# The correlation's gram in four groups of 32 tokens, two blocks in a row

## The chip, the cores and the metric

The kernel runs on one core of one Trainium2 chip, which works through all eight images by itself. The metric is the device time of one execution in microseconds, and the time of a kernel is the median of its runs.

## The reference, cut to what matters

The input `x` has 8 images of 768 channels by 32 x 32 positions (tokens), in float32. Two layers follow each other, each adding its result to its input.

```python
x = x + _L0_conv_ref(_gn(x), W_qkv, W_proj, b_proj)      # layer 0
    # qkv = tokens @ W_qkv.T ; 12 heads of 64
    # var_v, var_k = variance of v, k over the 64 of a head
    # attn = softmax(var_v @ var_k.T * 64**-0.5) ; out = attn @ v ; out @ W_proj.T + b_proj
x = x + _L1_conv_ref(_gn(x), conv_w, conv_b)             # layer 1
    # feat_n = feature / max(norm over channels, 1e-12), padded by 3 on each side
    # corr[o] = sum over channels of feat_n shifted by offset o, times feat_n
    #   28 offsets of a 7 x 7 window: diagonal, column, antidiagonal, row
    # out = conv_w (1x1) @ concat(feature, corr) + conv_b
```

`_gn` is a group normalisation over 32 groups. The change is in `corr`: each position's inner products over the 768 channels with its neighbours at up to three rows and three columns away.

## The kernel before, in words

**The order of the work.** The program is written out by Python. A planner (class `Clock`) keeps a planned time; every unit of matmuls passes it by a fixed number of microseconds (`KV_US` 1.93 for 12 matmuls of 384 columns, `STEP_US` 1.73 for one step of the attention, `GRAM_US` 1.4 for a gram block), and jobs for the other engines are put at a planned time with `later.after(us, job)`. That decides the order in which the instructions of each engine, and the DMAs of SP's one queue, stand. The engines run by that order and wait for each other's data by semaphores.

**The stages.** The loop `for b in range(NB + 1)` interleaves, in stage b, the attention of image b (layer 0) with the second half of its key and value products (`kv.units(1)`), and with the correlation and 1x1 convolution of image b-1 (layer 1). `work_off` takes attention steps when they are ready and units of the list `rest` otherwise; the gram blocks of image b-1 stand in a second list, `beside`, of which `next_to` starts one at two fixed places of `rest` and before and after each group of attention steps, and `remaining` what is left. The list `rest` then goes on with the convolution.

**The attention.** Twelve heads are six pairs. For each pair ACT makes the exponentials `ex` (L774) of 8 blocks of 128 tokens for both heads, from a row of values `bc` that SP loads as 512 KB (L763), and for some pairs it makes them once more in the other orientation only for their sums (`junk`, L784, from rows `bk`). TensorE multiplies them with the values (`av`, L800). Six `ex` buffers exist, three steps of two heads, so an exponential of step t+3 waits for the `av` of step t. Keys, values, projection and convolution are products by a scheme with fewer multiplications, recorded as `x`, `y`, `z`, `own` at L350; their sums of operands (`s`, L636 to L642) are made by POOL. For other pairs the denominators come from a product with ones, `den` (L831), with four groups of 32 columns.

**The correlation, class `Corr`.** A block is 128 tokens, that is 4 image rows of 32, and there are 8 blocks (`t`) to an image.

- `turn` (L1129 to L1142): POOL copies a block's features so that tokens of the left half of the image rows, and of the right, stand together: two copies of 128 x 384. The tile comes from a pool with one buffer (`turnpool`). Each gram turns the next block. The last image does it on ACT instead, two blocks ahead.
- `gram` (L1144 to L1181): for each of 6 channel slices and each side, one matmul with the turned tokens of that side (64) as the stationary operand and a window of 7 image rows by 19 columns (133; 76 for the last block, where the image ends) as the moving one. In float32 the profile shows each as two records, 24 for a block. The result `ps` is one of two PSUM buffers that it shares with the small transposes: `ptv`, `ptk` (the variances), `it`, `ct` (the correlation).
- `out`: DVE copies `ps` to `win`, and SP writes `win` to DRAM (`windowed`) in two DMAs, one for each side, each 4 image rows x 16 tokens x 136 elements, with a pitch such that a shift of the window becomes a fixed step.
- After blocks 3 and 7, `diagonals` (L1189) reads the products that are wanted back as four DMAs into `dd`, token by token; `scale` makes `m` (DVE) and the reciprocal root `rn` (POOL, L1205), `columns` makes `dn` (DVE), `to_dram` transposes it on TensorE (`ct`, L353), copies it (`cr`), and writes `rows` (L1226).
- `gather` (L1232): 14 DMAs read the rows and the shifted reciprocal norms into `cs` (named `u` in the code) and `v`, which has its own buffer (`uvpool`, 28 x 1024); `product` multiplies them, and three DMAs copy `cs` to the other partition groups. Convolution units then add `cs` with `cc` (L1276, and L1374 in the last image).

Of the kernel before, what the change touches and what calls it, by code (L numbers as in the profile page):

```python
# [6 lines left out]
F32 = mybir.dt.float32  # L7
AF = mybir.ActivationFunctionType
ALU = mybir.AluOpType
# [4 lines left out]
P = 128  # L14
NB, C, H, W = 8, 768, 32, 32
N = H * W
J = C // P
NH, HD = 12, 64
HP = NH // 2
MT = N // P  # L20
HF = N // 2
# [6 lines left out]
RUNS = ((0, 0, 4), (31, -1, 3), (62, -2, 5), (93, -3, 7))  # L28
HW = W // 2
TALL, WIDE = MT // 2 + 3, HW + 3  # L30
AHEAD_OF = [o for first, _, count in RUNS for o in range(first, first + count)][1:]
NA = len(AHEAD_OF)
PAD = 99
SPAN = TALL * WIDE
WIN = SPAN + 3
PITCH = WIN + 3
# [4 lines left out]
NS = len(CHANNELS)  # L41
NCH = 2 * NS + 4
# [11 lines left out]
TAIL = 0.0  # L54
EXP, SUM, STEP_US = 1.07, 1.15, 1.73
KV_US, T_US, CORR_US = 1.93, 2.58, 1.2
GRAM_US = 1.4
WARM, BRIDGE = 42, (3, 7)


# [26 lines left out]
def windows(ap, *dims):  # L87

    return bass.AP(tensor=ap.tensor, offset=ap.offset, ap=[list(d) for d in dims])


class Clock:


    def __init__(self):
        self.now, self.count, self.jobs = 0.0, 0, []
        self.act, self.rows, self.poll = 0.0, ([], []), lambda: None
        self.dve = 0.0

    def after(self, us, job):  # L100
        self.count += 1
# [71 lines left out]
def two_layers(ctx, tc, x, wkv, wproj, bproj, wconv, wcorr, bconv, out):  # L173
    nc = tc.nc

    def pool(name, bufs, **kw):
        return ctx.enter_context(tc.tile_pool(name=name, bufs=bufs, **kw))
# [10 lines left out]
    bcpool = pool("bcpool", 4)  # L188
    bkpool = pool("bkpool", 2)
    expool = pool("expool", 2 * AHEAD)  # L190
    turnpool = pool("turnpool", 1)
    wk = pool("wk", 3)
    uvpool = pool("uvpool", 1)
    st = pool("st", 1)
    xbank = pool("xbank", 2, space=PSUM)
    ybank = pool("ybank", 2, space=PSUM)
# [5 lines left out]
    clock = Clock()  # L202
    later = clock
    vector = Vector(nc.vector, clock)
    ready = set()
# [197 lines left out]
    for j in range(J):  # L403
        for hf, queue in enumerate((nc.sync, nc.scalar)):
            at = slice(hf * HF, (hf + 1) * HF)
# [18 lines left out]
    for base, sign in ((0, 1), (3, -1)):  # L424
        nc.gpsimd.affine_select(
            out=group, in_=group, compare_op=ALU.is_ge, fill=0.0, base=base,
# [16 lines left out]
    cs = const.tile([P, 3, HF], F32, name="cs")  # L443
# [681 lines left out]
    class Corr:  # L1125
# [3 lines left out]
        def turn(self, t):  # L1129
# [7 lines left out]
            for side in range(2):  # L1137
                if last:
                    act_copy(0.5, to[:, :, side], rows[:, :, :, side, :])
                else:  # L1140
                    half = rows[:, :, :, side, :]
                    nc.gpsimd.tensor_tensor(to[:, :, side], half, windows(ones, ones.ap[0], (0, J), (HW, 4), (1, HW)), ALU.mult)  # L1142

        def gram(self, t):  # L1144

            b = self.b
            tall = min(TALL, H - 4 * t)
            n = tall * WIDE
            if t not in self.turned:
                self.turn(t)  # L1150
            block = self.turned[t]
            ps = other([P, SPAN], f"gr{b}_{t}")
            for j in range(J):
                image = self.f[:, j, :].rearrange("p (y x) -> p y x", x=W)
                for side in range(2):
                    left = side * (HW - 3)
                    nc.tensor.matmul(  # L1157
                        ps[side * HD : (side + 1) * HD, :n].rearrange("p (y x) -> p y x", x=WIDE),
                        lhsT=block[:, j, side, :],
                        rhs=image[:, 4 * t : 4 * t + tall, left : left + WIDE],  # L1160
                        start=j == 0, stop=j == J - 1,
                    )
            for ahead in range(t + 1, min(t + (3 if b == NB - 1 else 2), MT)):
                if ahead not in self.turned:
                    self.turn(ahead)

            def out():
                win = wins[t % 2 if t < MT - 1 else 2]
                if b < NB - 1:
                    vector.tensor_copy(win[:, :n], ps[:, :n])  # L1170
                else:
                    act_copy(0.3, win[:, :n], ps[:, :n])
                for side in range(2):
                    to = windowed[b % 2][t : t + 1, side * (HD * PITCH + HD - 3) :]
                    nc.sync.dma_start(
                        out=windows(to, (HW * PITCH - 3, 4), (PITCH, HW), (1, WIN)), in_=win[side * HD : (side + 1) * HD, :]
                    )
                if t % 4 == 3:
                    later.after(4.0, lambda: self.diagonals(t // 4))

            later.after(GRAM_US + 0.25, out)  # L1181

        def diagonals(self, hf):

# [47 lines left out]
        def gather(self):  # L1232

            b, r = self.b, rows[self.b % 2]
            u = cs.rearrange("p a n -> p (a n)")[0:NCH, 0:N]
            v = uvpool.tile([NCH, N], F32, tag="uv", name=f"v{b}")
            nc.sync.dma_start(out=v[NS:NCH, :], in_=windows(r[0:1, PAD:], (0, NS + 4), (1, N)))
            nc.sync.dma_start(out=u[2 * NS : NCH, :], in_=windows(r[1:2, PAD:], (0, 4), (1, N)))
            for n, (first, apart) in enumerate(PICKED):
                k, row = 3 * n, 2 + AHEAD_OF.index(first)  # L1240
                nc.sync.dma_start(out=u[k : k + 3, :], in_=windows(r[row : row + 1, PAD:], (apart * ROW, 3), (1, N)))
                nc.sync.dma_start(out=v[k : k + 3, :], in_=windows(r[0:1, PAD + first :], (apart, 3), (1, N)))
                nc.sync.dma_start(
                    out=u[NS + k : NS + k + 3, :],
                    in_=windows(r[row : row + 1, PAD - first :], (apart * (ROW - 1), 3), (1, N)),
                )

            def product():
                vector.tensor_tensor(u, u, v, ALU.mult)
                vector.tensor_tensor(cs[0:NCH, 2, :], cs[0:NCH, 0, :], cs[0:NCH, 1, :], ALU.subtract)  # L1250
                for n in range(1, 4):
                    nc.sync.dma_start(out=cs[n * FOUR : n * FOUR + NCH, :, :], in_=cs[0:NCH, :, :])
                later.after_dve(6.0, lambda: ready.add(("cs", b)))

            later.after(18.0 if b < NB - 1 else 12.0, product)
# [136 lines left out]

    def remaining(beside):
        while beside:
            next_to(beside)

    def next_to(beside):

        if beside and ready.issuperset(beside[0][1]):
            us, _, unit = beside.pop(0)  # L1400
            unit()
            clock.pass_time(us)
# [19 lines left out]

    def turn_first():
        start_corr(0)
        later.after(6.0, lambda: ready.add("turned"))

    def project(b, ots, held=None):
        f = first_f[0] if b == 0 else layer1[b - 1][0]
# [110 lines left out]
    def start_corr(b):  # L1539
        corrs.append(Corr(b, layer1[b][0]))  # L1540
        corrs[-1].turn(0)

    second, corrs = [], []
    later.after(26.0, lambda: sum_weights(1, 9.0, 1.5))
# [4 lines left out]
    for b in range(NB + 1):  # L1549
# [8 lines left out]
        if b:  # L1558
            has_f = ("f", b - 1),
            if b > 1:  # L1560
                clock.wait(*has_f, ready=ready)
            f, acc = layer1[b - 1] if b > 1 else first_f * 2
            corr = corrs.pop() if 1 < b < NB else Corr(b - 1, f) if b == NB else None
            conv = Conv(
                b - 1, f, images[b] if b < NB else acc, (lambda b=b: next_image(b + 1)) if b + 1 < NB else lambda: None
            )
            if b < NB:

                def low_residual(b=b, f=f):
                    for n in range(JH):  # L1570
                        later.after(1.5 * n, lambda n=n: nc.sync.dma_start(out=f[:, n, :], in_=xv[b, :, n, :]))

                conv.then = low_residual
            grams = [(GRAM_US if t < MT - 1 else 0.9, has_f if b > 1 else has_f + ("turned",), lambda t=t: (corr or corrs[0]).gram(t)) for t in range(MT)]
            first, start = (0.0, has_f, conv.sums.first), (0.0, (), conv.start)
            if b < NB:
                beside = grams
                for n in (3, 7) if b > 1 else (7, 11, 15):
                    rest.insert(n, (0.0, has_f, lambda: next_to(beside)))
                rest.insert(len(rest) - 4, (0.0, has_f, lambda: remaining(beside)))  # L1580
                rest.insert(len(rest) - 4, first)
                rest += [start] + conv.units()
                if b == NB - 1:
                    rest.insert(len(rest) - 3, (0.0, (), conv.set_aside))
            else:
                units, parts = conv.units(), conv.corr_units()
                rest += [first, start] + units[:2] + grams + units[2:17]
                for n, unit in enumerate(units[17:]):
                    rest += parts[n : n + 1] + [unit]
        else:  # L1590
            more = [(us, (("xn", 1),) * (n > 1), unit) for n, (us, _, unit) in enumerate(kv1.units(0))]
            rest.insert(len(rest) - 3, (0.0, (), lambda: apply_second(0)))
            rest += [(0.0, (), lambda: apply_second(1))] + more[:20] + [(0.0, (), lambda: fill_t(3))] + more[20:]
            rest += [(0.0, (), lambda: fill_t(TBLOCKS - 3))]
# [51 lines left out]
```

## Time and profile before

| what | us |
|---|---|
| median of 3 runs | 2581.24 |
| lowest and highest | 2581.23, 2582.12 |
| profiled execution | 2580.07 |
| its span | 2578.3 |
| `gr` (L1157) on the chain that ended last | 3% of the span |
| turns on POOL, 112 copies | 111.0 |
| `win` copies on DVE, 56 | 16.1 |
| product of `cs` and `v` on DVE, 8 | 9.7 |

In the profile, PE is TensorE's matmuls, PEld its weight loads, DVE, ACT and POOL the other engines, and SPq the DMA queue of SyncE. The lines of a timeline have start, length, engine, line of the code, operation, output and inputs, their shapes and a count, and in brackets the idle time before them and what ended it. Matmuls overlap, so the length of a record is not its cost; from the start of a group to the start of the next is. A wait is put down to what came last.

### The profile page before, as it was taken

The numbers are of one execution on the slowest core, as the hardware profiler recorded it, in microseconds if no ns is written. First come the engines' busy times: TensorE is split into PE (matmuls) and PEld (weight loads), VectorE is DVE, ScalarE is ACT, GpSimd is POOL, SyncE is SP. The second block draws the span as 40 slices with busy tenths as digits, with TensorE's granted clock in tenths as the row PEclk, the third lists the DMA queues.
The fourth block names the chain that finished last, engine by engine and source line by source line (L and its number), as shares of the span: only waits on it lengthen the run. The fifth ranks groups of instructions, "written<-read, shape, count | busy, mean of one in ns | idle before, by whom it ended". The sixth has DMA issues, their size and how long they took to land.

```text
span 2578.3 us, 40707 instructions
## 1 busy us (share of the span) xinstructions
PE 2570.6 (100%) x14798; PEld 1345.3 (52%) x14798; DVE 1586.7 (62%) x4101; ACT 1422.0 (55%) x1972; POOL 425.3 (16%) x449
## 2 busy tenths in 40 slices
PE   9999999999999999999999999999999999999999
PEld 5644354434764347643476434764347643575333
DVE  6868735775347853478534885358853577536864
ACT  1497279811697217971179711897118971199610
POOL 4320130004300043000430003300133001331000
PEclk9999999999999999999999999999999999999999
DMA  8866366355563655636556365563655636545333
GB/s 295 291 225 221 103 210 189 119 196 170 184 200 104 198 169 175 206 97 208 168 174 202 98 212 171 168 201 105 221 170 162 206 107 218 163 142 166 119 110 108
DMA packets 324718, 448.19 MB, mean 174 GB/s; under 512 B 59810, under 2 KB 245522, under 8 KB 324518
## 3 DMA queue, kind: packets, MB, share of 16 engines
q1 hardware_dynamic: 322454, 442.24, 53.7%
q10 hardware_dynamic: 2064, 3.34, 0.4%
q8 instruction: 118, 1.93, 0.3%
q14 instruction: 82, 0.67, 0.1%
HBM read 376.70 MB, written 64.40 MB: 171 GB/s over the span
## 4 chain that ended last, share of the span: by engine, by line
PE 99%; DVE 0%; issue 0%; POOL 0%; DMA 0%; ACT 0%; SPq 0%; ACTq 0%; POOLq 0%; DVEq 0%
PE x L350 35%; PE av L800 25%; PE y L350 18%; PE z L350 10%; PE own L350 5%; PE gr L1157 3%; PE den L831 1%; PE warm L419 1%; PE y L1063 0%; PE z L1063 0%; PE cc L1276 0%; DVE acc L167 0%; DMA windowed<-win 0%; POOL turn L1142 0%; PE cc L1374 0%
## 5 line engine op out<-in xcount | busy, mean ns | idle before, releaser
L774 ACT ACTIVATE ex<-bc,nk 128x1024 f32<-128x1024 f32 x768 | 828.9, 1140 | 397.1 <-DMA bc<-vdr 191.0
L800 PE MATMUL av<-ex,v 128*64 128x512 f32 x3072 | 692.4, 593 | 0.1
L800 PEld LDWEIGHTS av<-ex,v 128*64 128x64 f32 x3072 | 337.1, 137 | 311.0 <-issue 182.3
L784 ACT ACTIVATE junk<-bk,vm 128x1024 bf16<-128x1024 f32 x368 | 421.5, 1145 | 26.9 <-issue 10.6
L167 DVE TENSOR_TENSOR acc<-acc,ex 128x1024 f32<-128x1024 f32 x300 | 344.9, 1214 | 0.0
L350 PE MATMUL y<-kv,s 128*64 128x384 f32 x1488 | 265.5, 487 | 0.7 <-POOL s L636 0.7
L350 PE MATMUL x<-kv,xn 128*64 128x384 f32 x1512 | 259.7, 486 | 0.0
L350 PE MATMUL x<-kv,s 128*64 128x384 f32 x1488 | 256.2, 486 | 0.0
L229 ACT COPY kp<-x 128x384 f32<-128x384 f32 x28 | 13.4, 479 | 404.6 <-PE x L350 395.8
L350 PEld LDWEIGHTS x<-kv,xn 128*64 128x64 f32 x1512 | 141.2, 137 | 102.4 <-issue 84.1
L350 PEld LDWEIGHTS x<-kv,s 128*64 128x64 f32 x1488 | 144.1, 137 | 91.6 <-issue 70.5
L350 PEld LDWEIGHTS y<-kv,s 128*64 128x64 f32 x1488 | 139.3, 137 | 87.7 <-issue 70.9
L530 POOL TENSOR_TENSOR rstda<-vea,neghalf 128x1 f32<-128x1 f32 x8 | 4.8, 596 | 947.5 <-DVE vea L167 947.5
L1142 POOL TENSOR_TENSOR turn<-f,ones 128x384 f32<-128x384 f32 x112 | 111.0, 1011 | 242.1 <-PE gr L1157 153.5
L350 PE MATMUL z<-kv,xn 128*64 128x384 f32 x768 | 134.1, 486 | 0.0
L350 PE MATMUL x<-f,wt 128*64 128x512 f32 x504 | 118.5, 593 | 0.0
L167 DVE TENSOR_TENSOR v<-y,v 128x128 f32<-128x128 f32 x180 | 41.0, 284 | 122.9 <-PE y L350 122.9
L636 POOL TENSOR_TENSOR s<-xn 128x384 f32<-128x384 f32 x64 | 66.6, 1051 | 294.0 <-PE x L350 189.1
L167 DVE BATCH_NORM_STATS2 vbn<-v 128x6 f32<-128x64 f32 x720 | 101.9, 213 | 0.0
L350 PEld LDWEIGHTS z<-kv,xn 128*64 128x64 f32 x768 | 75.9, 137 | 46.4 <-issue 36.6
L229 ACT COPY acc<-li 32x256 f32<-32x256 f32 x128 | 51.7, 404 | 82.8 <-DVE li L167 81.4
L1157 PEld LDWEIGHTS gr<-f,turn 128*64 128x64 f32 x1344 | 89.6, 136 | 11.0 <-POOL turn L1142 1.3
(205 smaller groups left out, 3134.0 us busy)
## 6 DMA issues: line engine op xcount, KB each, us to landing
kv<-kvs SPq DMA_DIRECT2D x124, 576.0 KB
kv<-in_wkv_dram SPq DMA_DIRECT2D x95, 576.0 KB
bc<-vdr SPq DMA_DIRECT2D x96, 512.0 KB
f<-in_x_dram SPq DMA_DIRECT2D x48, 512.0 KB
bk<-kdr SPq DMA_DIRECT2D x46, 512.0 KB
x1d<-f SPq DMA_DIRECT2D x42, 512.0 KB
xn<-x1d SPq DMA_DIRECT2D x42, 512.0 KB
out_dram<-xn SPq DMA_DIRECT2D x82, 256.0 KB
```

Source lines behind the costliest of these rows:

```text
L167: return getattr(self.engine, name)(*args, **kw)
L229: nc.scalar.copy(to, at)
L350: nc.tensor.matmul(out[at], lhsT=lhsT[:, at], rhs=rhs, start=start, stop=stop, **kw)
L419: nc.tensor.matmul(warm[:, 0:P], lhsT=ident, rhs=ident, start=True, stop=True)
L530: nc.gpsimd.tensor_tensor(self.rstd, ve, neghalf[:, 0:1], ALU.pow)
L636: nc.gpsimd.tensor_tensor(self.sums[g][:, 0], a[g][2], a[g][3], ALU.add)
L774: nc.scalar.activation(ex, self.bc[e], AF.Exp, scale=self.kv.nk[self.half][:, h, t : t + 1])
L784: nc.scalar.activation(junk, self.bk[e], AF.Exp, scale=self.kv.m2[self.half][:, h, t : t + 1], accum_out=self.sums[:, e, t : t + 1],)
L800: nc.tensor.matmul(self.av[hf][e * HD : (e + 1) * HD, :], lhsT=self.vt[:, t, e, :], rhs=exs[e][:, hf * HF : (hf + 1) * HF], start=t == 0, ...
L831: nc.tensor.matmul(den[at * 32 : (at + 1) * 32, :], lhsT=ones[:, 0:32], rhs=self.acc[e][:, hf * HF : (hf + 1) * HF], start=True, stop=True,)
L1142: nc.gpsimd.tensor_tensor(to[:, :, side], half, windows(ones, ones.ap[0], (0, J), (HW, 4), (1, HW)), ALU.mult)
L1157: nc.tensor.matmul(ps[side * HD : (side + 1) * HD, :n].rearrange("p (y x) -> p y x", x=WIDE), lhsT=block[:, j, side, :], rhs=image[:, 4 * ...
```

## The change

For images 0 to 6 the block of 128 tokens is multiplied in four groups of 32 instead of two of 64: the left and right halves of two image rows each. A group's window needs 5 image rows instead of 7, so the moving operand has 95 columns, and there are twice as many matmuls. The four groups' results stand in four groups of 32 partitions of `ps`, that is in four column groups of the array. Block 7 keeps its 76 columns. The eight blocks are started as four pairs, and a `turned` time in the planner keeps a pair from being started before two turns have had time. There are two turn buffers; turns run two ahead. The window's DMAs are four to a block of 2 image rows x 16 tokens x 98 elements, except for block 7 (two, as before). The tile `v` is now two halves of 512 columns that lie in the two turn buffers, so five loads of the gather become ten, and the product is two multiplications. The last image keeps its two groups and takes over only the halves of `v`. Image 0's grams stand at other places of `rest`.

```diff
+SHORT = 2 + 3
-GRAM_US = 1.4
+GRAM_US, TURN_US = (1.3, 2.4), 3.4
...
-    turnpool = pool("turnpool", 1)
+    turnpool = pool("turnpool", 2)
-    uvpool = pool("uvpool", 1)
...
+        def grams(self, t):
+            clock.turned = clock.now + GRAM_US[1] + TURN_US
+            for n in range(2):
+                self.gram(t + n)
...
+            last = t == MT - 1
+            groups = 2 if b == NB - 1 else 4
+            tall = min(SHORT if groups == 4 else TALL, H - 4 * t)
...
-                for side in range(2):
-                    left = side * (HW - 3)
+                each = P // groups
+                for at in range(groups):
+                    side, low = divmod(at, groups // 2)
+                    left, first = side * (HW - 3), 4 * t + (0 if last else 2 * low)
                     nc.tensor.matmul(
-                        ps[side * HD : (side + 1) * HD, :n].rearrange("p (y x) -> p y x", x=WIDE),
-                        lhsT=block[:, j, side, :],
-                        rhs=image[:, 4 * t : 4 * t + tall, left : left + WIDE],
+                        ps[at * each : (at + 1) * each, :n].rearrange("p (y x) -> p y x", x=WIDE),
+                        lhsT=block[:, j, side, low * each : (low + 1) * each],
+                        rhs=image[:, first : first + tall, left : left + WIDE],
                         start=j == 0, stop=j == J - 1,
                     )
-            for ahead in range(t + 1, min(t + (3 if b == NB - 1 else 2), MT)):
+            for ahead in range(t + 1, min(t + 3, MT)):
...
-                for side in range(2):
-                    to = windowed[b % 2][t : t + 1, side * (HD * PITCH + HD - 3) :]
+                whole = last or groups == 2
+                size, count, down = (WIN, 4, 0) if whole else (SHORT * WIDE + 3, 2, 2 * (HW * PITCH - 3 + WIDE))
+                for first in range(0, P, count * HW):
+                    side, low = divmod(first, HD)
+                    to = windowed[b % 2][t : t + 1, side * (HD * PITCH + HD - 3) + (down if low else 0) :]
...
-            later.after(GRAM_US + 0.25, out)
+            later.after(1.65 if b == NB - 1 else GRAM_US[t % 2] + 0.25, out)
...
-            v = uvpool.tile([NCH, N], F32, tag="uv", name=f"v{b}")
-            nc.sync.dma_start(out=v[NS:NCH, :], in_=windows(r[0:1, PAD:], (0, NS + 4), (1, N)))
+            vs = [turnpool.tile([P, J * P], F32, tag="turn", name=f"v{b}_{hf}") for hf in range(2)]
+            for hf, v in enumerate(vs):
+                nc.sync.dma_start(out=v[NS:NCH, :HF], in_=windows(r[0:1, PAD + hf * HF :], (0, NS + 4), (1, HF)))
...
-                vector.tensor_tensor(u, u, v, ALU.mult)
+                for hf, v in enumerate(vs):
+                    vector.tensor_tensor(cs[0:NCH, hf, :], cs[0:NCH, hf, :], v[0:NCH, :HF], ALU.mult)
...
+            clock.turned = 0.0
             next_to(beside)
...
-        if beside and ready.issuperset(beside[0][1]):
+        if beside and ready.issuperset(beside[0][1]) and clock.now >= clock.turned:
...
-        later.after(6.0, lambda: ready.add("turned"))
+        later.after(8.0, lambda: ready.add("turned"))
...
         corrs[-1].turn(0)
+        corrs[-1].turn(1)
...
-                for n in (3, 7) if b > 1 else (7, 11, 15):
+                for n in (3, 7) if b > 1 else (7,) + tuple(range(12, 30, 2)):
```

More of the change, by code (lines that the diff above doesn't have):

```diff
@@ L97, in __init__ @@
         self.act, self.rows, self.poll = 0.0, ([], []), lambda: None
-        self.dve = 0.0
+        self.dve = self.turned = 0.0
     def after(self, us, job):
@@ L1142, in turn @@
                     nc.gpsimd.tensor_tensor(to[:, :, side], half, windows(ones, ones.ap[0], (0, J), (HW, 4), (1, HW)), ALU.mult)
+        def grams(self, t):
+            clock.turned = clock.now + GRAM_US[1] + TURN_US
+            for n in range(2):
+                self.gram(t + n)
         def gram(self, t):
             b = self.b
-            tall = min(TALL, H - 4 * t)
+            last = t == MT - 1
+            groups = 2 if b == NB - 1 else 4
+            tall = min(SHORT if groups == 4 else TALL, H - 4 * t)
             n = tall * WIDE
@@ L1172, in out @@
                     act_copy(0.3, win[:, :n], ps[:, :n])
-                for side in range(2):
-                    to = windowed[b % 2][t : t + 1, side * (HD * PITCH + HD - 3) :]
+                whole = last or groups == 2
[3 more added lines that the diff above has]
+                    to = windowed[b % 2][t : t + 1, side * (HD * PITCH + HD - 3) + (down if low else 0) :]
                     nc.sync.dma_start(
-                        out=windows(to, (HW * PITCH - 3, 4), (PITCH, HW), (1, WIN)), in_=win[side * HD : (side + 1) * HD, :]
+                        out=windows(to, (HW * PITCH - 3, count), (PITCH, HW), (1, size)),
+                        in_=win[first : first + count * HW, :size],
                     )
@@ L1241, in gather @@
                 nc.sync.dma_start(out=u[k : k + 3, :], in_=windows(r[row : row + 1, PAD:], (apart * ROW, 3), (1, N)))
-                nc.sync.dma_start(out=v[k : k + 3, :], in_=windows(r[0:1, PAD + first :], (apart, 3), (1, N)))
+                for hf, v in enumerate(vs):
+                    nc.sync.dma_start(out=v[k : k + 3, :HF], in_=windows(r[0:1, PAD + first + hf * HF :], (apart, 3), (1, HF)))
                 nc.sync.dma_start(
@@ L1248, in product @@
             def product():
-                vector.tensor_tensor(u, u, v, ALU.mult)
+                for hf, v in enumerate(vs):
+                    vector.tensor_tensor(cs[0:NCH, hf, :], cs[0:NCH, hf, :], v[0:NCH, :HF], ALU.mult)
                 vector.tensor_tensor(cs[0:NCH, 2, :], cs[0:NCH, 0, :], cs[0:NCH, 1, :], ALU.subtract)
@@ L1573, in two_layers @@
                 conv.then = low_residual
-            grams = [(GRAM_US if t < MT - 1 else 0.9, has_f if b > 1 else has_f + ("turned",), lambda t=t: (corr or corrs[0]).gram(t)) for t in range(MT)]
+            if b < NB:
+                keys = has_f if b > 1 else has_f + ("turned",)
+                grams = [(GRAM_US[1], keys, lambda t=t: (corr or corrs[0]).grams(t)) for t in range(0, MT, 2)]
+            else:
+                grams = [(1.4 if t < MT - 1 else 0.9, has_f, lambda t=t: corr.gram(t)) for t in range(MT)]
             first, start = (0.0, has_f, conv.sums.first), (0.0, (), conv.start)
```

## The prediction

> **What bounds the kernel now.** I read the busy row and the chain first. The page's head gives a span of 2578.3 us; the profiled execution took 2580.07 us, 1.8 us around the span, and 1.2 us less than the median, 2581.24. The sum below is made against the 2580.07 and then moved up by 1.2. The granted clock is 1.000.
>
> ```profile
> PE 2570.6 (100%) x14798; PEld 1345.3 (52%) x14798; DVE 1586.7 (62%) x4101; ACT 1422.0 (55%) x1972; POOL 425.3 (16%) x449
> PE 99%; DVE 0%; issue 0%; POOL 0%; DMA 0%; ACT 0%; SPq 0%; ACTq 0%; POOLq 0%; DVEq 0%
> ```
>
> By these, TensorE is everything, and a microsecond taken from it is a microsecond gained. Averages can hide a stage in which a second engine is just as full, so next I read busy time by stretches of one stage (image 3's attention; stages repeat every 318.3 us). Columns: length, then PE, PEld, DVE, ACT, POOL busy, clock, DMA share, GB/s. Then the ACT waits of the first stretch (sum, count, longest), and the two long ones in the ACT timeline (start, length, ..., idle before).
>
> ```profile
> 989.00:1083.10 94.10, 94.10 (x599) 68.61 (x595) 41.05 (x166) 90.15 (x121) 20.16 (x21) 1.00 0.57 180
> 1083.10:1160.00 76.90, 76.90 (x372) 38.86 (x370) 50.71 (x52) 62.46 (x73) 0.00 (x0) 1.00 0.36 112
> ```
> ```profile
> ACT ex L774 <- PE av L800: 3.4, 3, 2.2
> ```
> ```profile
> 991.16 3.24 ACT L774 ACTIVATE ex<-bc,nk 128x1024 f32<-128x1024 f32 x3 [2.19 <-PE av L800]
> ```
> ```profile
> 1006.49 2.19 ACT L774 ACTIVATE ex<-bc,nk 128x1024 f32<-128x1024 f32 x2 [0.93 <-PE av L800]
> ```
>
> From the first `av` (989.0) until the exponentials of the third head pair end (1083.03), ACT works through: 90.15 of 94.10 us, and of the rest it waits 3.4 us in three places for a buffer that an `av` frees. PE reaches the `av` that consumes the last of these within 0.5 us of it. So this stretch has two full engines, and all eight gram blocks lie in it or just ahead of it. After 1083.1 ACT is idle 14.4 of 76.9 us and only PE counts.
>
> **The grams.** A block before is 24 matmul records of 133 columns:
>
> ```profile
> 987.66 1.57 PE L1157 MATMUL gr<-f,turn 128*64 128x133 f32 x23
> 989.02 0.59 PE L800 MATMUL av<-ex,v 128*64 128x512 f32 x1
> ```
> ```profile
> 1030.76 1.05 PE L1157 MATMUL gr<-f,turn 128*64 128x76 f32 x23
> 1031.63 0.49 PE L350 MATMUL x<-kv,s 128*64 128x384 f32 x1
> ```
>
> Start to start, 989.02 - 987.66 = 1.36 us (113 ns for each pair side by side); the short block 0.87. A stage has 7 x 1.36 + 0.87 = 10.4 us of it. After, a block is 48 records of 95 columns, in sets of four. The nearest row of the old trace is the denominators' `den`, 32 columns wide and four side by side:
>
> ```profile
> 525.39 2.85 PE L350 MATMUL y<-f,wt 128*64 128x512 f32 x12
> 528.18 1.06 PE L831 MATMUL den<-acc,ones 128*32 128x512 f32 x8
> 529.17 2.37 PE L350 MATMUL x<-f,wt 128*64 128x512 f32 x10
> ```
>
> Its two sets take 0.99 us from entry to leaving, where two streams of 512 columns take 0.79 to 0.85; singly read starts put the extra cost of going to 32 columns and back at 0.205 us. A pair of blocks then costs 24 sets x (95/133 x 110.8 + 2.5 = 82 ns) + 0.205 = 2.17 us against 2.72, and the last pair, whose second block keeps 76 columns, 1.98 against 2.23. Three pairs and the last save 3 x 0.55 + 0.25 = 1.9 us a stage.
>
> A rule speaks against this: the Trainium skill, "TensorE: Matmul & The Clock Gate", section "Wait — 56ns, not 53.3ns?", says that starts come no closer than about 25 ns, however few columns. Four starts per set would then make 100 ns, not 82, and the pair 24 x 100 + 205 = 2.6 us, saving 0.1. The old trace does not decide: `den` starts its four 7 ns apart, but then rests 430 ns; the densest sustained row is the 76-column block, one start per 33 ns, and that is what its own columns need. If 33 ns were the floor, a pair would take 3.4 us. The other rule, "TensorEngine Tiling (Array Packing)", section "Key Properties", has a change of tiling drain the array; the row prices that at 0.205 us, and running two blocks in a row pays it four times a stage rather than eight. I take P = 2.25 us for a pair, nearest to `den`, and keep 2.1 to 2.6 for the range.
>
> **What the shorter grams are worth in one stage.** The order of both programs' instructions shows the move. Count from T, where the values' transposes start (971.12 here). Before the first `av`: was 3 blocks, 0.4 of transposes and 7 units of 12 matmuls at 1.93, i.e. 4.08 + 0.4 + 13.5 = 17.9 us, as measured (989.02). Now 3 pairs, 0.4 and 6 units: 3P + 12.0, which is 18.45 at P = 2.17 and 18.7 at 2.25. So the first `av` comes 0.5 + 3(P - 2.17) later, and with it ACT's start at 991.16. In return the fifth `av` (t4) is reached sooner: before at 1004.41 = T + 33.3; now four steps of 1.715, transposes `ct` 0.3, last pair 1.98 and two units 3.87 after the first one, i.e. T + 31.5. ACT's wait of 0.93 us there goes. The end of ACT's run thus moves by 0.5 - 0.93 + 3(P - 2.17) = -0.4 + 3(P - 2.17): -0.2 us at P = 2.25, -0.6 at 2.1, +0.3 at 2.4, +0.9 at 2.6. PE, which has 1.6 us less to do, would wait for exponentials (about 0.7 us at the first pair's t7, 0.3 at each of the next two): that is what is late next. Six stages (images 1 to 6): -1.2 us.
>
> Image 0's grams run in a stage where ACT is full too; there PE lost 0.24 and 0.23 us to the single turn tile (`gr` waits for `turn`, 0.5 in all), which a second tile removes. Beyond that, ACT could run on only if its row loads come sooner, too; I take -0.8, between 0 and -1.5. Image 7 keeps its grams.
>
> **The other parts.** *Turns*: POOL does the same 16 of 1.97 us each, two ahead; after the ones that follow the maximum at 968.6 it starts at 976.26. By walking the queue, turns 2 and 3 end at T + 9.1 and PE wants them at T + 9.5: 0.4 us of cover. POOL is 16% busy; moving turns ahead of the `s` sums pushes these by 2 to 4 us, under the conv's later use: nothing. *Copies and windows*: eight copies of 0.29 us on DVE as before; SP issues 14 more window DMAs an image, each 16 rows lower but half as many; SP's queue, about 0.3 us an issue, has room except where named below. *Gather and product*: five more loads (0.31 us each on SP = 1.6 us) and the product as two halves of about 0.6 us where one took 1.21; its result is due tens of us later in images 0 to 6. In image 7 the copies of `cs` are now landed by my count near 2559.6 against a use at 2560.45: 0, or +0.8 at worst. *The v tile's own buffer* goes; the turn tiles are idle by then, since the next image's first turn comes a stage later: 0.
>
> Sum: 2580.07 - 1.2 - 0.8 = 2578.1, plus 1.2 to the median: **2579 us**.
>
> **Rivals.** *The gain is kept* (chance 0.17): if ACT's run isn't what ends the stretch, because its waits shrink further when `av` comes sooner, PE's saving stays: 6 x 1.9 + 1.5 = 13 us, 2568. For it: PE busy 100%, chain 99%. Against: the 90.15 of 94.10.
>
> *The windows stand behind the row loads* (0.16, slower). Grams 2 and 3 now come earlier and in a row, and their eight window DMAs stand in SP's queue behind four row loads (`bk`, `bc`, 512 KB each) and ahead of the diagonals, so `dn` is late and PE stands at the first `ct`, now put right after four `av` steps:
>
> ```profile
> 981.83 0.88 SPq L763 DMA_DIRECT2D bk<-kdr  x2
> 982.76 1.42 SPq L763 DMA_DIRECT2D bc<-vdr  x2
> ...
> 1002.05 2.02 SPq L1189 DMA_DIRECT2D dd<-windowed  x4
> ```
>
> Before, `dn` was done at 1008.9 and used at 1012.6, 3.7 us of cover. My walk of the new order has it done at T + 25.05 against a use at T + 25.3: 0.25 left. A wait of x behind that holds `av` t4 and all PE work behind it; the first 1.3 us replace PE's waits for ACT. It breaks even at x = 1.5 and at x = 3 costs 1.7 - 0.2 = 1.5 us in six stages, +9: 2590 us. For it: the windows and the loads meet; against: the planner gave `dn` the same fixed delays, and 2 MB are mostly landed by then.
>
> *Starts are the limit* (0.14): P = 2.6 by the rule gives +0.9 x 6 - 0.8 = +5, 2586; at 2.9, 2591. *It doesn't do what it says*, i.e. four groups run two by two: 48 x 82 ns would be 4 us a pair and +30 us; `den`'s four records within 0.43 us speak against it (0.02).
>
> **How the numbers follow.** ACT-bound, as summed: 0.51, with 2574 to 2584. A measurement of this kernel can tell about 0.2%, 5.2 us, from no change. Faster than 2576: the kept gain 0.17 and 0.08 of the likeliest case, 0.25. Slower than 2586.4: 0.14 of the windows, 0.09 of the starts, 0.02, and 0.02 of the likeliest, 0.27. The rest, 0.48. The range reaches from 2570, in between the likeliest and the kept gain, to 2589, which leaves out some 0.1 on each side.
>
> **What would show it.** A pair of blocks start to start near 2.25 us and its records in fours; 82 ns or 100 ns a set decides the rule. ACT's waits in the stretch: the 0.93 gone, the 2.2 larger by 0.5 to 0.8; new waits of `av` for `ex` on PE, about 1.3 us a stage. `ct` waiting for `dn` shows the slower rival. A stage that shrinks by 1.9 us with no PE wait would prove me wrong about ACT, and one that grows with P at 2.2 wrong about SP's queue.

## The result, and the profile after

The changed kernel takes 2624.18 us (median of 6 runs, 2622.47 to 2629.13) against 2581.23 (2579.92 to 2582.12): a ratio of 1.0171, 95% interval 1.0161 to 1.0182, 43 us slower. I had said 2579, and 2570 to 2589. The profiled execution took 2628.18 us with a span of 2626.5; 5.0 us of its surplus lie ahead of the first image's transposes, where its granted clock was one half for 6.8 us as in no other profiled run, and have no part in what follows.

Busy time and chain first:

```profile
PE 2585.6 (98%) x16142; PEld 1188.4 (45%) x16142; DVE 1599.3 (61%) x4109; ACT 1418.1 (54%) x1972; POOL 421.9 (16%) x449
PE 90%; DMA 4%; DVE 3%; ACT 1%; SPq 1%; issue 1%; POOL 0%; DVEq 0%; ACTq 0%
```

PE's part of the chain was 99% before; it has left a tenth of it to others, above all DMA and DVE. Its waits (us in total, times, longest) name the place; before, all its waits together were under 4 us:

```profile
PE ct L353 <- DVE dn L168: 27.6, 12, 3.8
PE ct L353 <- DVE win L168: 3.0, 1, 3.0
```

The twelve waits for `dn` are two in each of the six stages of images 1 to 6. PE's timeline of image 2's correlation, in the stage that the prediction read:

```profile
1000.08 2.17 PE L1167 MATMUL gr<-f,turn 128*32 128x95 f32 x96
1002.18 7.09 PE L800 MATMUL av<-ex,v 128*64 128x512 f32 x32
1012.62 0.69 PE L353 MATMUL ct<-ident,dn 128*64 128x128 f32 x4 [3.35 <-DVE dn L168]
1013.24 2.97 PE L1167 MATMUL gr<-f,turn 128*32 128x95 f32 x96
1016.14 2.16 PE L350 MATMUL y<-kv,s 128*64 128x384 f32 x12
```

The pair of gram blocks takes 1002.18 - 1000.08 = 2.10 us. Behind four `av` steps PE stands 3.35 us at `ct`. The next pair, one of whose blocks is shorter, takes 2.90 us. The windows around it say why (length, busy times, granted clock, DMA share, GB/s):

```profile
1008.00:1012.00 4.00, 1.27 (x6) 0.14 (x2) 0.81 (x5) 4.00 (x6) 1.06 (x1) 0.99 0.30 13
1012.00:1016.00 4.00, 3.38 (x100) 3.09 (x100) 1.02 (x6) 3.97 (x6) 0.00 (x0) 0.58 0.10 24
1016.00:1020.00 4.00, 4.00 (x40) 1.80 (x30) 1.69 (x10) 2.54 (x5) 0.00 (x0) 1.00 0.09 22
```

After standing, PE runs at half its clock. Apart from the drop at the start, the clock record has one at the first `ct` of every stage from image 0 to image 6: five of 3.4 us and two of 6.8 us; before there was none inside the span. What `dn` waited for is in SP's queue:

```profile
994.20 2.75 SPq L1188 DMA_DIRECT2D windowed<-win  x4
996.99 0.91 SPq L763 DMA_DIRECT2D bk<-kdr  x2
998.09 1.79 SPq L763 DMA_DIRECT2D bc<-vdr  x2
1000.03 2.43 SPq L1188 DMA_DIRECT2D windowed<-win  x4
1008.16 2.03 SPq L1203 DMA_DIRECT2D dd<-windowed  x4
```

Gram 3 was done at 994.1. Its windows were issued at 1000.03, behind gram 2's and the 2 MB of row loads, and `dd`, which reads them back, could only start at 1008.16. Before, `dd` could start at 1002.05, with gram 3's windows issued 4.1 us ahead of it:

```profile
997.95 1.09 SPq L1175 DMA_DIRECT2D windowed<-win  x2
```

And ACT, of which I had said that it would be what PE meets, waits more for PE rather than less (6.8 us from the first `av` to 1100, against 3.4 in the stretch before):

```profile
ACT ex L774 <- PE av L800: 6.8, 3, 3.4
```

### The profile page after: what moved, and what is told of

It reads as the page before. It is cut to its first block, busy times and chain, and to the rows that moved or that the text cites. A ratio compares the mean times of both kernels' runs of the same rounds, so it can differ in the third digit from the quotient of the medians.

```text
span 2626.5 us, 43625 instructions
## 1 busy us (share of the span) xinstructions
PE 2585.6 (98%) x16142; PEld 1188.4 (45%) x16142; DVE 1599.3 (61%) x4109; ACT 1418.1 (54%) x1972; POOL 421.9 (16%) x449
## 4 chain that ended last, share of the span: by engine, by line
PE 90%; DMA 4%; DVE 3%; ACT 1%; SPq 1%; issue 1%; POOL 0%; DVEq 0%; ACTq 0%
PE x L350 34%; PE av L800 22%; PE y L350 17%; PE z L350 9%; PE own L350 5%; PE gr L1167 2%; DMA windowed<-win 2%; DVE dn L168 1%; PE den L831 1%; DMA dd<-windowed 1%; ACT ex L774 1%; DMA xn<-in_x_dram 0%; DVE v L168 0%; DVE acc L168 0%; DMA bc<-vdr 0%
## 5 line engine op out<-in xcount | busy, mean ns | idle before, releaser
L800 PE MATMUL av<-ex,v 128*64 128x512 f32 x3072 | 704.8, 595 | 1.0 <-ACT ex L774 0.6
L800 PEld LDWEIGHTS av<-ex,v 128*64 128x64 f32 x3072 | 289.3, 137 | 374.3 <-issue 277.4
L350 PEld LDWEIGHTS x<-kv,s 128*64 128x64 f32 x1488 | 133.9, 137 | 107.1 <-issue 95.7
L350 PEld LDWEIGHTS x<-kv,xn 128*64 128x64 f32 x1512 | 119.7, 137 | 125.9 <-issue 111.0
L350 PEld LDWEIGHTS y<-kv,s 128*64 128x64 f32 x1488 | 123.1, 138 | 106.3 <-issue 92.0
L350 PE MATMUL x<-f,wt 128*64 128x512 f32 x504 | 124.2, 593 | 0.0
L168 DVE SCALAR_TENSOR_TENSOR xn<-x,bconv_sb,xn 128x512 f32<-128x512 f32 x63 | 46.4, 745 | 89.4 <-PE x L350 88.8
L350 PEld LDWEIGHTS z<-kv,xn 128*64 128x64 f32 x768 | 64.1, 137 | 60.6 <-issue 50.1
```

What stands on the lines that cost most here:

```text
L168: return getattr(self.engine, name)(*args, **kw)
L350: nc.tensor.matmul(out[at], lhsT=lhsT[:, at], rhs=rhs, start=start, stop=stop, **kw)
L800: nc.tensor.matmul(self.av[hf][e * HD : (e + 1) * HD, :], lhsT=self.vt[:, t, e, :], rhs=exs[e][:, hf * HF : (hf + 1) * HF], start=t == 0, ...
```

## The experiments

The theory after the result: **the loss is the two waits at `ct` and the clock behind the first; they come from the windows' place in SP's queue and from the row loads beside them**. Rivals: the narrow tiles or the narrow windows cost by themselves; the order of the grams and ACT's later start cost; the clock falls for another reason. All times below are medians; the kernel before had 2580.5 to 2581.0 beside them.

**1. Row loads behind gram 3's windows.**

```diff
+                if hp == 1 and self.b > 1 and ("win", self.b - 1) not in ready:
+                    return
...
                 if t % 4 == 3:
+                    ready.add(("win", b))
```

> The changed kernel; only the two bk and two bc row loads of the second head pair (2 MB) are issued behind the windows of gram 3, not ahead of them, for images 1 to 6. Theory A (windows land late because they stand behind the row loads, dn is late, PE stands 3.4 us at the first ct and its clock halves for 3.4 us after that): dn done 4 to 6 us earlier, the first ct waits under 0.5 us, no clock drop in six stages: 2624 - 6 x (3.4 + 1.7) = about 2593, and 2590 to 2598 as the second ct keeps its 1.2 us. Theory B (four window DMAs to a block and 392-byte pieces are slow by themselves, or ct simply stands too early): dn moves by under 1.5 us, the first ct still waits over 2 us: 2612 to 2626.

Measured: 2600.46 us (ratio 1.008, 1.0063 to 1.0096). The edit moved less than I had written: the two `bk` loads belong to the first pair and stayed ahead, so 1 MB of the 2 MB moved. `dn` came 2.4 us earlier, the first `ct` waited 0.6 to 2.05 us (none in one stage), and no clock drop was left in the six stages:

```profile
PE ct L353 <- DVE dn L168: 15.7, 11, 2.0
```

The time is above theory A's 2590 to 2598, and the sizes are smaller than it had them. Its direction holds: with half of the traffic moved, the first waits fell from 19.4 to 7.1 us in sum. Theory B's 2612 to 2626 is out.

**2. `ct` later.**

```diff
-                later.after_dve(0.7 if b else 5.0, lambda: to_dram(dn))
+                later.after_dve(0.7 + (b < NB - 1) * 9.0 if b else 5.0, lambda: to_dram(dn))
```

> The changed kernel with to_dram, and so both ct, planned 9 us later for images 1 to 6 (the first ct now stands between the fifth and sixth av step after the first four). If the waits at ct and the clock drops behind them are the whole loss: no PE wait at ct in six stages, clock 1.000 there, 2624 - 6 x (4.5 + 1.7) = about 2587, and with the 1.1 us a stage that DVE's order costs (v<-v,rd ahead of the first acc) still there. Rival: the loss is in the new order of the grams and ACT's later start, and PE meets ACT instead: 2600 to 2615, waits of av for ex in place of ct for dn.

Measured: 2584.62 us (2581.08 to 2590.16; ratio 1.0017, 1.0009 to 1.0025). No wait at `ct` in the six stages, and 39.6 of the 43 us are gone, though `dn` is as late as in the changed kernel (28.8 us after the values' transposes). PE doesn't meet ACT in their place.

**3. The four groups in the old order.** The kernel before, with the matmuls and the narrow windows of the change only; the diff is the core of it, and the lines that follow from it are those of the change.

```diff
+            groups = 2 if b == NB - 1 else 4
+            tall = min(SHORT if groups == 4 else TALL, H - 4 * t)
...
```

> The kernel before with the four groups of 32 columns and their short windows only: blocks stay single and where they were, one turn tile, v as before. A block should take 12 x 79 ns + 0.2 = 1.15 to 1.2 us against 1.36, so PE loses 1.2 us of work a stage. ACT-bound theory: the first av comes 0.5 us sooner and the end of the stretch follows by 0.3 to 0.6: 2577 to 2580. Gain-kept theory: 7 x 1.2 = 8 us, 2573. Slower theory (narrow tiles or 14 more window DMAs an image cost by themselves): dn late, ct waits, over 2586.

Measured: 2578.35 us (ratio 0.9992, 0.9983 to 1.0). PE's timeline:

```profile
988.38 1.19 PE L1162 MATMUL gr<-f,turn 128*32 128x95 f32 x48
989.50 7.09 PE L801 MATMUL av<-ex,v 128*64 128x512 f32 x32
```

A single block is 1.12 us to the next start, against 1.36, and yet each stage is only 0.37 us shorter. The time lies where the ACT-bound theory had it, but PE itself gives the gain back, around each block. The neighbours of these two blocks, first before the change, then here:

```profile
985.72 2.26 PE L350 MATMUL y<-kv,s 128*64 128x384 f32 x12
995.88 1.57 PE L1157 MATMUL gr<-f,turn 128*64 128x133 f32 x23
```
```profile
986.34 2.10 PE L351 MATMUL y<-kv,s 128*64 128x384 f32 x12
996.51 1.19 PE L1162 MATMUL gr<-f,turn 128*32 128x95 f32 x48
```

The unit ahead of the block takes 2.04 us instead of 1.94, and the four `av` steps between two blocks 7.01 instead of 6.86. A pair of blocks pays this once instead of twice. Neither the narrow tiles nor four window DMAs a block make a loss where they meet nothing: `dn` is done 37.2 us after the transposes, before the change 37.8.

**4. Two groups in the new order.**

```diff
-            groups = 2 if b == NB - 1 else 4
+            groups = 2
```

> The changed kernel with two groups of 64 columns and the two wide window DMAs again; order of work, two blocks in a row, two turn tiles, halves of v stay. A pair costs 2.7 us against 2.1. If the order makes the loss, the first ct still waits 2 to 4 us and the clock still drops: 2624 + 6 x 1.9 = about 2635 (2628 to 2640). If the four narrow window DMAs make it, the waits go: 2624 - 31 + 11 = about 2604.

Measured: 2598.54 us (ratio 1.0072, 1.0057 to 1.0087), below all that I had expected. PE's waits at `ct` for `dn`:

```profile
PE ct L353 <- DVE dn L168: 6.1, 6, 1.4
```

All six are at the second `ct` of a stage. The first one finds `dn` ready, in image 2 by 0.6 us, and the clock never drops. So the order alone takes the cover away and makes the second wait; the first wait needs the four groups in that order. In image 2 they bring `dn` 2.7 us later and PE 1.3 us sooner to `ct`. The windows' part in this: gram 2's two wide ones occupy SP for 1.2 us where the four narrow ones took 2.75; with two the row loads leave sooner, and gram 3's windows are issued at 14.0 rather than 16.6. My "if the order makes the loss" and "if the narrow windows make it" were both too simple; with experiment 3, neither does it without the other.

**5. Windows past SP's queue.**

```diff
-                    nc.sync.dma_start(
+                    (nc.gpsimd if t == 3 and 0 < b < NB - 1 else nc.sync).dma_start(
```

> The changed kernel with the four window DMAs of gram 3 of images 1 to 6 issued by POOL, past SP's queue. If the place in SP's queue is what delays them (behind two bk and two bc loads and gram 2's windows), they start 2 to 3 us sooner and dn is done 2 to 3 us earlier: first ct waits 0.5 to 1.5 us, no clock drop: about 2598 to 2605. If they are slow to land because 2 MB of row loads hold the DMA engines meanwhile, or POOL issues slowly, dn moves by under 1 us: 2618 to 2628.

Measured: 2607.44 us (ratio 1.0102, 1.0089 to 1.0115). POOL issued the four at 991.12, 13.8 us after the transposes:

```profile
991.12 2.60 POOL L1188 DMA_DIRECT2D windowed<-win  x4
```

`dn` came 2 us earlier, the first `ct` waited 0.4 to 1.7 us.

```profile
PE ct L353 <- DVE dn L168: 20.3, 12, 2.6
```

The time is 2 us above the 2605 that I had at most: the second `ct` now waits 1.6 to 2.65 us, and the clock drops behind it in three of the six stages. Passing the queue gives 2 us of `dn`; each window still took 5 to 7 us from issue to landing, and the read-back started 6.9 us after the last issue; before the change it was 3.5. Both are in it, the place in the queue and the slow landing.

That the row loads slow the landing, and not the small pieces of the narrow windows, is read from the other experiments in the same stage. In experiment 1, with half of the loads moved behind, the read-back starts 3.7 us after the last issue. In experiment 4 the two wide windows stand beside the loads, and it is 7.4 us; in experiment 3 the four narrow ones are clear of them, and it is 2.5.

One stage of each kernel (image 2's grams), in us after the values' transposes:

```
                      gram 3 copied   windows issued   dd issued   dn done   ct on PE
before                    26.5          26.8-27.4        30.9        37.8      41.5
changed                   11.2          16.6-18.4        24.7        29.0      29.2
1 rows behind             11.0          13.6-16.9        20.7        26.6      26.7
3 four, old order         26.0          26.3-28.1        30.6        37.2      41.1
4 two, new order          11.9          14.0-14.6        22.0        26.3      26.9
5 POOL's queue            11.7          13.8-15.8        22.7        27.0      27.2
```

**6. The wait filled.** Four matmuls whose result is overwritten stand ahead of the first `ct` (they add work and change no output).

```diff
                 pt = small(f"ct{b}_{hf}")
+                for n in range(4 if hf == 0 and 0 < b < NB - 1 else 0):
+                    nc.tensor.matmul(pt, lhsT=ident, rhs=self.f[:, 0, 0:HF], start=True, stop=True)
```

> The changed kernel with four idle matmuls of 128x512 (3.4 us, their result is overwritten) on PE right ahead of the first ct of images 1 to 6, where PE waited 2.3 to 3.8 us. PE is as late as before but busy. If the halved clock after the wait is a consequence of PE's idling, the clock stays 1.000 in six stages and the time falls by what the drops cost, 6 x 1.7 to 3.4 = 10 to 14 us: 2610 to 2615. If the drop comes from something else (load of other engines, DMA), it stays: 2624 or a little more.

Measured: 2620.02 us (ratio 1.0152, 1.0139 to 1.0165).

```profile
1004.63 3.70 PE L1231 MATMUL ct<-f,ident 128*128 128x512 f32 x8
1008.26 0.44 PE L353 MATMUL ct<-ident,dn 128*64 128x128 f32 x4
1008.63 1.98 PE L1167 MATMUL gr<-f,turn 128*32 128x95 f32 x96
```

No clock drop is left in the six stages, and the last pair is back at 1.91 us from 2.90: the idling causes the drop. But the time fell by 4, not 10 to 14 us. The filler is 0.4 us longer than the mean wait, and PE, no longer slowed, reaches the second `ct` sooner and stands there 1.8 us in the mean where it was 1.4: part of what the half clock cost lay ahead of another wait. In the profiled executions the six stages fell by 5.3 us, and the drop at image 0's `ct`, which has no filler, was 6.8 us long instead of 3.4.

**7. DVE's order as well.** In experiment 2 the stages of images 1 to 5 gained 0.6 to 1.4 us up to the first of two `den`, against the kernel before, and each gave back 1.13 between the two. There DVE's order had moved. Before:

```profile
1119.19 1.21 DVE L167 TENSOR_TENSOR v<-v,rd 128x1024 f32<-128x1024 f32 x1
1125.00 0.69 DVE L167 TENSOR_TENSOR xn<-z,xn 128x512 f32<-128x512 f32 x1 [4.60 <-PE z L1063]
1127.52 2.35 DVE L167 TENSOR_TENSOR acc<-ex,ex 128x1024 f32<-128x1024 f32 x2
```

After the change:

```profile
1142.39 0.69 DVE L168 TENSOR_TENSOR xn<-z,xn 128x512 f32<-128x512 f32 x1 [5.73 <-PE z L1063]
1144.91 1.22 DVE L168 TENSOR_TENSOR v<-v,rd 128x1024 f32<-128x1024 f32 x1
1146.05 2.35 DVE L168 TENSOR_TENSOR acc<-ex,ex 128x1024 f32<-128x1024 f32 x2
```

`v<-v,rd` used to fill an idle stretch; now it stands behind the `xn` operations and ahead of the `acc` that frees ACT's buffers. Nothing in the change names it: the planner's times moved.

```diff
-            self.rd_at = clock.now + {HP // 2: 8.0, HP - 2: 12.0}.get(self.hp, 14.0)
+            self.rd_at = clock.now + {HP // 2: 8.0, HP - 2: 12.0, HP // 2 - 1: 12.0 if self.b else 14.0}.get(self.hp, 14.0)
...
-                later.after_dve(0.7 if b else 5.0, lambda: to_dram(dn))
+                later.after_dve(0.7 + 9.0 * (b < NB - 1) if b else 14.0, lambda: to_dram(dn))
```

> The run with ct later, with two more moves in the plan: the rows for the third head pair count as landed 2 us earlier, which puts v<-v,rd back ahead of the four xn operations in DVE's order as in the kernel before (images 1 to 6), and image 0's ct stand 9 us later as well. If DVE's order costs 1.1 us a stage (the step of +1.13 between two den in each stage) it goes: -6.7 us, and -2 to -4 for image 0's wait of 2.3 us and its clock drop: 2571 to 2577, below both kernels. If ACT is the hidden bound (my prediction's step), the stage cannot shrink below that of before by more than 0.2 to 0.6 us: 2577 to 2582.

Measured: 2582.94 us over 22 runs from 2577.38 to 2591.93 (ratio 1.0009, 1.0003 to 1.0016): a miss in the median, of which I had expected 2571 to 2577. In the profiled execution the step between the `den` is gone; two of the stages are 1.4 us shorter than before, two 0.8 to 0.9. But one is 3.5 us longer. PE's timeline there, and POOL's:

```profile
1656.42 5.78 PE L350 MATMUL y<-kv,s 128*64 128x384 f32 x24 [2.47 <-POOL s L640]
```
```profile
1650.02 1.01 POOL L1219 TENSOR_TENSOR rn<-m,neghalf 128x4 f32<-128x4 f32 x1 [16.12 <-DVE m L168]
1651.00 1.96 POOL L636 TENSOR_TENSOR s<-xn 128x384 f32<-128x384 f32 x2
1652.92 1.95 POOL L638 TENSOR_TENSOR s<-s,xn 128x384 f32<-128x384 f32 x2
1654.83 1.96 POOL L640 TENSOR_TENSOR s<-xn,s 128x384 f32<-128x384 f32 x2
```

The second half's `rn`, which waits for a DMA, stands in POOL's queue ahead of the `s` sums, and PE for `s`; then the clock drops again.

**8. The same with two groups.** Experiment 7 with `groups = 2`.

> The same as the run above it with two groups of 64 columns (and two wide window DMAs) instead of four of 32. If the shorter grams are kept once nothing waits: slower than that run by 7 blocks' worth, 6 to 7 stages x 1.5 = 9 to 11 us, 2580 to 2588. If ACT bounds the stretch, the two differ by 1 to 4 us only, since ACT takes back what PE gains.

Measured: 2583.37 us (2582.49 to 2584.5; ratio 1.0008, 1.0 to 1.0016). The medians differ by 0.4 us, less than either case had, and taken alone would speak for ACT. But experiment 7 has that wait for `s`, and this run has none at L640; by stages the two differ: +0.14 us each in this run against before, -1.39 and -1.40 in the two best stages of experiment 7. The four groups are worth 1.53 us a stage, and in such a stage all of it is kept.

**9. The sums ahead of `rn`.** Experiment 7 with

```diff
-            later.after(6.0, lambda: self.scale(hf, dd))
+            later.after(6.0 + 8.0 * (hf == 1 and b < NB - 1), lambda: self.scale(hf, dd))
```

> The run with ct later and DVE's order mended, with one more move: the scale of blocks 4 to 7 is planned 8 us later (images 0 to 6), so that POOL's rn of that half, which waits for a DMA, stands behind the s sums in POOL's queue as before the change, not ahead of them. If PE's wait of 2.5 us for s in one stage of that run (and a clock drop of 3.4 us behind it) came from this, no stage waits for s at L640, the spread of its times (2577 to 2592) shrinks to some 3 us, and the time is 6 stages x -1.4, with about +1 elsewhere: 2571 to 2576. If the spread has another source (row loads, ACT), it stays, and the median with it near 2580 to 2583.

Measured: 2571.75 us (2571.02 to 2574.62; ratio 0.9966, 0.9954 to 0.9979), 9 us below the kernel before and 52 below the changed one. No wait for `s` at L640. Against before, the first five stages are -1.4 us three times, -0.32 and -1.23, and the sixth runs like the first three as far as its first `it`. The stretch in which I had called ACT full, over the same 94.10 us from its first `av`, and ACT's waits for `av` there:

```profile
986.42:1080.52 94.10, 94.10 (x595) 56.05 (x593) 43.91 (x169) 92.61 (x125) 13.45 (x15) 1.00 0.61 187
```
```profile
ACT ex L774 <- PE av L800: 0.4, 1, 0.4
```

## Why the prediction was wrong, by its steps

**The cost of a pair (right).** 2.10 us to the next start, and units after and before the pair 0.04 and 0.1 us longer: 2.24 with both, where I took 2.25. The first `av` came 18.71 us after the transposes; I had 18.7. A set of four starts every 81.7 ns. That is the line through the old blocks, 113.3 ns a set for 133 columns and 65.9 for 76, at 95 columns. The rule that spoke against it does not hold here: 81.7 ns are 20.4 ns a start, below the 25 that the Trainium skill, "TensorE: Matmul & The Clock Gate", section "Wait — 56ns, not 53.3ns?", gives as the least. The section "Measured speedup vs the span model" of the same page, some 4 ns for each further tile, would have come nearer: 79 ns of columns and 3 x 4 make 91 ns as an estimate, where the other rule makes 100.

**ACT's bound (wrong by 1.2 us a stage).** I let only one of ACT's waits, 0.93 us, give way, and put the stage at -0.2 (for P = 2.25). Experiments 7 and 9 have -1.4 in their best stages, experiment 8 at P = 2.72 has +0.14 where the same formula says +1.25. The slope was right (1.53 us where 3 x 0.47 gives 1.4), the level was not: ACT's waits for `av` were PE's pace showing on ACT, and they shrank from 3.4 to 0.4 us in experiment 9. An engine that is busy for 96% of a stretch and waits only for the bound engine is not a second bound. The rival "the gain is kept" had the mechanism, for a program in which nothing else moves.

**PE's waits for ACT (wrong, and they mattered).** With them I had cushioned the slower rival: "the first 1.3 us replace PE's waits for ACT". In experiment 9, where nothing else holds PE, the whole run has two of them, 0.8 us in all, so each microsecond at `ct` counts.

**The windows behind the row loads (the step that failed; the rival that came, mis-sized).** The sum put this wait at nothing. The rival's place and mechanism were right; `dn` I had at 25.05 us after the transposes, and it was done at 27.9 in image 1 and at 28.8 to 29.6 in images 2 to 6, while PE reached `ct` at 25.8. The term that failed is "2 MB are mostly landed by then": the windows were themselves issued only at 16.6 to 18.4 (image 2), because the loads and gram 2's four windows fill SP's queue until then (for 1.1 us of it SP waits for an earlier load), and the read-back could start only 6 us after the last of them, beside the loads. For a wait of 3 us I had +9 us in all; the mean wait of 3.2 us with nothing to cushion it makes 19.

**What the prediction did not have.** The clock: PE's standing halves it for 3.4 or 6.8 us, which cost 1.2 to 2.8 us a stage. The second `ct`, 1.4 us a stage; experiment 4 has it from the order alone (1.0 us). The order on DVE. The order on POOL, which I had called nothing ("under the conv's later use"); in the changed kernel PE waits 0.4 us for `s` in all, in experiment 7 2.5 us in one stage. Image 0's stage, for which I had -0.8, got 2.1 us longer, with 3.0 of wait at `ct` for a `win` copy that waits for a window DMA.

**The sum over images 1 to 6**, from the profiled executions: first `ct` 19.4, second 8.2, half clock 11.0, DVE's order 5 x 1.13 = 5.7, grams -6 x 1.4 = -8.4: 35.9 of 40.0 measured. The 11.0 is the time from the first `ct` to the second, without the wait at its end, over the 19.04 us that it is in images 2 to 6 of experiment 1, where the clock does not drop; half of the drops' length would be 13.6, but some began while PE still stood. Image 0 adds 2.1, the end 1.4. The 4.1 left over, some 0.7 us a stage, isn't explained; the same sum for image 2 leaves it in experiments 1 and 4 too. Not separated is which of the loads delays a window, and how.

## What to carry to other kernels

When work is pulled forward, its consumers are pulled forward too: compare the slack of each chain that starts there (here gram, copy, DMA out, DMA back, transpose) with the new distance, and count the queue's issue time and whatever large load lands beside it. In a program whose order is planned by estimated times, changing one duration reorders engines that the change does not touch, so compare the order of all of them. An engine that waits only for the bound engine is not itself a bound.

## What the runs showed of the hardware

A PE idle time of 2.3 to 3.8 us at the first `ct` came, in each of the stages of images 1 to 6 of the changed kernel, with a granted clock of one half for 3.4 or 6.8 us; in some stages the drop began before the wait had ended. In experiment 1, waits of up to 2.05 us brought none in these stages; in experiment 5, waits of 2.06, 2.53 and 2.65 us at the second `ct` did, and one of 2.34 did not; in experiment 6, none of those of up to 2.5 us did. The Trainium skill, "TensorE: Matmul & The Clock Gate", section "What's actually happening", speaks of a free-running window of about 3.4 us and of an idle one; the lengths of the drops agree, and idle times clearly shorter than the window were enough here.

Four matmuls in four groups of 32 columns, with 95 columns moving, start every 82 ns as a set for a whole pair of blocks. Going from tiles of 64 columns to these and back costs about 0.15 us: the units ahead of a pair and behind it take 0.1 and 0.04 us longer.
